# Dealing sums, weight products, LayerNorm and MLP steps out between tile products, and all of their transfers onto one queue in that order

## The chip, the cores and the metric

One core of a Trainium2 chip. The runs were made in batches, each on one chip with the kernel before beside it. The metric is the device time of one execution in microseconds, given as the median of the timed runs.

## The reference, cut to what matters

Two images of 256 channels, 128 x 128, float32. Three branches (dilations 1, 9, 12) each take offsets from a 3x3 convolution, sample the image bilinearly at 9 displaced taps, weight the samples per channel, sum, and apply LayerNorm and GELU. Their sum goes through a 1x1 convolution's addition, LayerNorm, a two-layer MLP and a second LayerNorm. A ternary 3x3 convolution follows.

```python
def _branch(x, w_off, w_def, lw, lb, pad, dil):
    off = _conv(x, w_off, pad, dil)
    y = _deform_dw(x, off, w_def, pad, dil)          # bilinear samples, 9 taps, summed
    return gelu(_ln2d(y, lw, lb))
x1 = _branch(x, off_w1, def_w1, bw1, bb1, 1, 1)
x2 = _branch(x, off_w2, def_w2, bw2, bb2, 9, 9)
x3 = _branch(x, off_w3, def_w3, bw3, bb3, 12, 12)
c = einsum('bchw,oc->bohw', x, conv_w) + conv_b
out = _ln2d(x1 + x2 + x3 + c, n1_w, n1_b)
h = gelu(out @ mlp_w1.T + mlp_b1) @ mlp_w2.T + mlp_b2
out = _ln2d(h + out, n2_w, n2_b)
# ... residual, group norm, ternary 3x3 convolution, residual
```

## The kernel before: the parts that matter

Sampling is a matrix product here: a tile of image rows (`xs`) times a matrix of interpolation weights (`A`). A is a product too: one factor is loaded by DMA straight into A, the other into `hy`, and VectorE (DVE) multiplies them in place. This is called a build below.

```python
def load_columns(u):                                 # A's first factor, 3 loads per unit
    for ky in taps(u):
        src, at, n = hat_rows(u, ky, TR, [[HY * 3 * W, TC], [0, TR]])
        pin(nc.scalar.dma_start(k["A"][u % 2][0:PT, AO + at : AO + at + n], src))

def build():                                         # A *= hy on DVE
    hy, u, at, n = hys.popleft()
    A = k["A"][u % 2][0:PT, AO + at : AO + at + n]
    pin(nc.vector.tensor_tensor(A, A, hy[0:PT, 0:n], ALU.mult))
    following = next(ahead, None)
    if following:
        load_rows(*following)                        # the next hy

def sample(u, c):                                    # unit u, channel half c
    # ...
    due = len(taps(u + 1)) if c == 0 and u + 1 < len(units) else 0
    last = c == KC - 1 and u + 2 < len(units)
    # ...
    ev = pool.tile([P, 9 * RI, NT * CI], F32, name="ev", tag="ev", bufs=2)
    for T in range(0, NT, 2):                        # 9 pairs of tiles
        if T // 2 % (NT // 2 // SLOTS + 1) == 0:     # at 3 places
            tail.advance()
        pm = psum.tile([P, 2, 256], F32, name="pm", tag="pm", bufs=4)
        # ... two products into pm on TensorE (PE), one copy pm -> ev on ScalarE (ACT)
    if last:
        load_columns(u + 2)
    sums = ev.rearrange("p (q i t) x -> p q i t x", q=3, t=3)
    for ky in kys:
        accumulate(u, c, sums, ky)                   # ring += w * ev on DVE, some 3 operations each
        for _ in range(due):
            build()                                  # unit u+1, after the first ky
        due = 0
```

A finished group of four rows goes through a chain of steps (transposes and statistics, normalising, transposing back, GELU, 1x1 convolution, MLP). Each chain is a generator; `yield n` asks to be continued at least n places later. `Tail.advance` is called at a place and runs one step of every chain that is due:

```python
def advance(self):
    self.now += 1
    # ... perhaps begin a waiting chain
    for item in list(self.running):
        if item[0] <= self.now and self.may(item):
            n = next(item[1], None)
            # ... remove the chain, or set item[0] = self.now + n
```

Three steps of a chain have a DVE operation that needs a result of PE or ACT from the same step:

```python
# normalised(): 4 transposes on PE, copied by ACT into T, then
nc.vector.bn_stats(st[:, j, :], Tv[:, j, :])
# finish(), first part: 1x1 convolution on PE into pc, then
nc.vector.scalar_tensor_tensor(S[:, m, :], pc, convb[:, m : m + 1], S[:, m, :], ALU.add, ALU.add)
# finish(), later: second MLP product on PE into h2, then
nc.vector.scalar_tensor_tensor(S[:, m, :], h2, b2[:, m : m + 1], S[:, m, :], ALU.add, ALU.add)
```

`pin` holds an instruction in program order on its engine; without it the scheduler may move it. Before, SyncE's transfers are not pinned.

## Time and profile before

| | before |
|---|---|
| time, median of 3 | 8016.15 us |
| sampling stage | 5779 us |
| PE busy in it, and idle | 5048, 731 us |
| DVE busy in it, and idle | 4536, 1243 us |
| PE waiting for ACT's copies | 565 us |
| DVE waiting for a finished sample | 862 us |

The stage rows come from the windows view, the waits from the groups by line; both are printed in the prediction. In the groups by line, the numbers after the bar are busy time and mean ns of one, then the idle time of the engine just before these instructions and what ended most of it.

```profile
L675 DVE TENSOR_TENSOR A<-A,hy 126x1152 f32<-126x1152 f32 (+2 forms) x752 | 970.9, 1342 | 37.9 <-DMA hy<-hats 20.8
```

The 752 builds cost DVE 971 us of work, and almost no waiting: their data is there when their turn comes.

### The profile page before, as it was taken

The numbers are of one execution on the slowest core, as the hardware profiler recorded it, in microseconds if no ns is written. First come the engines' busy times: TensorE is split into PE (matmuls) and PEld (weight loads), VectorE is DVE, ScalarE is ACT, GpSimd is POOL, SyncE is SP. The second block draws the span as 40 slices with busy tenths as digits, with TensorE's granted clock in tenths as the row PEclk, the third lists the DMA queues.
The fourth block names the chain that finished last, engine by engine and source line by source line (L and its number), as shares of the span: only waits on it lengthen the run. The fifth ranks groups of instructions, "written<-read, shape, count | busy, mean of one in ns | idle before, by whom it ended". The sixth has DMA issues, their size and how long they took to land. (4 is left out here: it accounts for less than half of the span.)

```text
span 7990.8 us, 100817 instructions
## 1 busy us (share of the span) xinstructions
PE 7025.9 (88%) x33648; PEld 5284.3 (66%) x33648; DVE 6010.1 (75%) x11183; ACT 4350.3 (54%) x8530; POOL 625.5 (8%) x1292
## 2 busy tenths in 40 slices
PE   5999878988888888888888898889888888699999
PEld 3555577777777777777677777777777776344444
DVE  7666578788778878877678778887787876577676
ACT  2344356666666666666656666666666666333232
POOL 0000000111111111111100111110111111000000
PEclk9999899999999999999999999999999999799999
DMA  8777677777677767766577767766776765222121
GB/s 299 208 194 192 172 245 242 220 233 230 222 219 220 234 213 227 229 213 204 181 230 239 226 220 230 234 220 217 226 226 213 233 213 160 75 81 73 69 79 49
DMA packets 833608, 1579.92 MB, mean 198 GB/s; under 512 B 96496, under 2 KB 492232, under 8 KB 828720
## 3 DMA queue, kind: packets, MB, share of 16 engines
q1 hardware_dynamic: 710384, 1106.97, 44.7%
q10 hardware_dynamic: 122688, 466.35, 18.5%
q8 instruction: 270, 4.42, 0.2%
q14 instruction: 266, 2.18, 0.1%
HBM read 1306.71 MB, written 266.36 MB: 197 GB/s over the span
## 5 line engine op out<-in xcount | busy, mean ns | idle before, releaser
L754 PE MATMUL pm<-A,xs 126*128 126x216 f32 (+2 forms) x17952 | 3570.0, 354 | 644.8 <-ACT ev L763 564.7
L754 PEld LDWEIGHTS pm<-A,xs 126*128 126x128 f32 x17952 | 3285.8, 199 | 922.2 <-ACT ev L763 688.3
L763 ACT COPY ev<-pm 128x432 f32<-128x432 f32 (+2 forms) x4752 | 2087.7, 492 | 1094.2 <-PE pm L754 709.1
L716 DVE SCALAR_TENSOR_TENSOR ring<-ev,defw,ring 128x384 f32<-128x384 f32 (+5 forms) x4376 | 2388.6, 568 | 130.6 <-ACT ev L763 28.5
L675 DVE TENSOR_TENSOR A<-A,hy 126x1152 f32<-126x1152 f32 (+2 forms) x752 | 970.9, 1342 | 37.9 <-DMA hy<-hats 20.8
L712 DVE TENSOR_SCALAR ring<-ev,defw 128x384 f32<-128x384 f32 (+2 forms) x568 | 305.8, 546 | 862.4 <-ACT ev L763 862.3
L480 ACT ACTIVATE T<-T,rs 128x256 f32<-128x256 f32 x1280 | 662.0, 599 | 6.8 <-POOL rs L476 6.8
L508 ACT ACTIVATE T<-zc,bb,bw 128x512 f32<-128x512 f32 x384 | 277.4, 774 | 621.4 <-DMA A<-hats 253.7
L1078 PE MATMUL pc<-cring,signs 128*128 128x512 bf16 x2304 | 520.9, 385 | 57.6 <-DVE signs L966 24.9
L1078 PE MATMUL pc<-cring,sums 128*128 128x512 bf16 x2304 | 510.3, 380 | 0.0
L473 POOL TENSOR_SCALAR rs<-mv 128x4 f32<-128x4 f32 x320 | 81.4, 254 | 5313.7 <-DVE mv L471 3889.3
L439 PE MATMUL hp<-T,w 128*128 128x512 f32 x1024 | 487.9, 600 | 9.1 <-ACT T L559 8.6
L469 DVE BATCH_NORM_STATS2 st<-T 128x6 f32<-128x256 f32 x1280 | 445.2, 411 | 59.1 <-ACT T L461 59.0
L203 PE MATMUL pz<-wz,xa 128*128 128x486 f32 x1024 | 459.1, 581 | 1.9 <-DVE zr L210 1.9
L439 PE MATMUL h<-hT,w 128*128 128x512 f32 x1024 | 460.0, 592 | 0.0
L1078 PEld LDWEIGHTS <-signs 128*128 128x128 bf16 x2304 | 227.1, 99 | 340.7 <-issue 44.4
L461 ACT COPY T<-tp 128x512 f32<-128x512 f32 x640 | 344.2, 597 | 196.8 <-PE tp L459 189.7
L1078 PEld LDWEIGHTS <-sums 128*128 128x128 bf16 x2304 | 225.4, 98 | 274.4
L492 PE MATMUL zc<-ident,T 128*128 128x128 f32 x2560 | 358.6, 287 | 29.9 <-ACT T L480 15.9
L492 PEld LDWEIGHTS zc<-ident,T 128*128 128x128 f32 x2560 | 319.1, 149 | 98.5 <-issue 39.6
L1062 ACT CAST cring<-D 128x2048 bf16<-128x2048 f32 x128 | 243.3, 1901 | 223.2 <-PE pc L1078 153.0
L572 ACT ACTIVATE hT<-hp,b 128x512 f32<-128x512 f32 x256 | 175.7, 687 | 339.2 <-PE hp L439 246.0
(119 smaller groups left out, 5722.7 us busy)
## 6 DMA issues: line engine op xcount, KB each, us to landing
A<-hats ACTq DMA_DIRECT2D x736, 567.0 KB
hy<-hats SPq DMA_DIRECT2D x736, 567.0 KB
xs<-table SPq DMA_DIRECT2D x1496, 126.0 KB
g12d<-T SPq DMA_DIRECT2D x128, 512.0 KB
other<-g12d SPq DMA_DIRECT2D x128, 512.0 KB
hats<-hb SPq DMA_DIRECT2D x192, 240.0 KB
hats<-hb SPq DMA_DIRECT2D x192, 192.0 KB
xl<-x1d SPq DMA_DIRECT2D x56, 640.0 KB
```

The lines of the kernel that those rows point to most:

```text
L203: nc.tensor.matmul(pz[:, 0:NZ], lhsT=xt[:, c, r, :], rhs=k["wz"][:, c, :], start=c == 0, stop=c == KC - 1,)
L439: nc.tensor.matmul(out, lhsT=w, rhs=v, start=i == 0, stop=i == n - 1)
L461: nc.scalar.copy(Tv[:, 2 * h : 2 * h + 2, :].rearrange("p j c -> p (j c)"), tp)
L469: pin(nc.vector.bn_stats(st[:, j, :], Tv[:, j, :]))
L480: nc.scalar.activation(Tv[:, j, :], Tv[:, j, :], AF.Identity, scale=rs[:, 0, j : j + 1], bias=rs[:, 1, j : j + 1],)
L492: nc.tensor.transpose(zc[:, j * P : (j + 1) * P], Tv[:, j, c * P : (c + 1) * P], ident)
L675: pin(nc.vector.tensor_tensor(A, A, hy[0:PT, 0:n], ALU.mult))
L712: pin(nc.vector.tensor_scalar(dst, src, w, None, ALU.mult))
L716: nc.vector.scalar_tensor_tensor(dst, src, w, dst, ALU.mult, ALU.add)
L754: nc.tensor.matmul(pm[:, j, 0:n], lhsT=xts[b, Rt][T + j][0:PT, c * P : (c + 1) * P], rhs=rhs, start=True, stop=True,)
L763: nc.scalar.copy(ev[:, q0 * 3 : q1 * 3, T * CI : (T + nt) * CI].rearrange("p m (t j) -> p t m j", j=CI), pm[:, 0:nt, 0:n].rearrange("p t ( ...
L1078: nc.tensor.matmul(pc[:, bank, :], lhsT=w[:, m * P : (m + 1) * P], rhs=xc[:, i, k, t * JC : (t + 1) * JC, kx : kx + W], start=j == 0, stop ...
```

## The change

The intent: PE, ACT and DVE should all have work between any two pairs of products, with no lump of sums and no several chain steps in one place. ACT should issue no transfers, so that its copies are never held. The core of the diff:

```diff
-NORMS = 3
+NORMS = 4
+XAHEAD = 4
-GAP = 2
-SLOTS = 3
+GAP = 4
         def advance(self):
-            for item in list(self.running):
+            for item in self.running:
                 if item[0] <= self.now and self.may(item):
                     ...
+                    return                          # one step of one chain
+        def load(self, tile, src):                  # every transfer of a chain
+            self.pin(nc.sync.dma_start(tile, src))
 ...  (load_columns)
-                pin(nc.scalar.dma_start(k["A"][u % 2][0:PT, AO + at : AO + at + n], src))
+                pin(nc.sync.dma_start(k["A"][u % 2][0:PT, AO + at : AO + at + n], src))
 ...  (load_rows)
-            nc.sync.dma_start(hy[0:PT, 0:n], src)
+            pin(nc.sync.dma_start(hy[0:PT, 0:n], src))
 ...  (sample, inside the loop over 9 pairs, after the products and the copy)
+                if following:                       # the next row tile's xs, pinned, one by one
+                    ...
+                            load_tile(*following, i + XAHEAD)
+                for _ in range(-(-len(pending) * 2 // (NT + 1 - T))):
+                    pending.popleft()()             # sums and builds of the sample before
+                tail.advance()                      # at all 9 places
 ...  (after the loop)
+            if kys:
+                pending.extend(sums(u, c, ev))
+            if c == KC - 1:
+                if u + 2 < len(units):
+                    load_columns(u + 2)
+                    pending.extend([build] * len(taps(u + 2)))
```

In the chains the waits grew (`yield 5` to `yield 8` before normalising, a new `yield 3` before the statistics, `yield 2` before both additions above, and others). A's load is issued at the end of a unit, and its build is dealt out within the very next sample, where before it came only after that sample, behind its first sums.

## The prediction

> **What bounds the kernel now.** I read the page's totals first, then the chain of waits, then the windows by stage.
>
> ```profile
> PE 7025.9 (88%) x33648; PEld 5284.3 (66%) x33648; DVE 6010.1 (75%) x11183; ACT 4350.3 (54%) x8530; POOL 625.5 (8%) x1292
> ...
> issue 7%; PE 6%; DVE 0%; DMA 0%; POOL 0%; POOLq 0%
> ```
>
> No engine is full, and the chain covers only the last stage (the 3x3 convolution). It says nothing of the stage that the change touches. Windows cut at the first and last tile product (953 and 6732 us) and at the last convolution's start do:
>
> ```profile
> core 0: us, PE busy (x) PEld busy (x) DVE busy (x) ACT busy (x) POOL busy (x), PEclk, DMA share, GB/s
> 0.00:953.00 953.00, 829.28 (x3400) 465.44 (x3400) 622.65 (x1345) 346.45 (x641) 3.42 (x9) 0.98 0.76 217
> 953.00:6732.00 5779.00, 5047.96 (x25159) 4291.42 (x25160) 4536.49 (x8706) 3591.71 (x7527) 589.85 (x1212) 0.95 0.71 222
> 6732.00:6904.00 172.00, 136.27 (x476) 73.27 (x474) 71.35 (x206) 95.68 (x171) 30.45 (x68) 0.88 0.25 80
> 6904.00:7991.00 1087.00, 1012.43 (x4616) 454.15 (x4616) 779.61 (x928) 316.46 (x192) 1.81 (x3) 0.96 0.20 71
> ```
>
> The second row is the sampling stage: 5779 us, 72% of the span. PE is idle for 5779 - 5048 = 731 us of it, DVE for 1243. The third row is the drain of the last chains. The stage has 2 images x 44 row tiles x 3 branches = 264 units of 2 samples (one per channel half), so 528 samples of 10.95 us. Each sample is 9 pairs of tile products, copied out by ACT, then summed by DVE.
>
> The groups by line and the waits say what PE and DVE wait for:
>
> ```profile
> L754 PE MATMUL pm<-A,xs 126*128 126x216 f32 (+2 forms) x17952 | 3570.0, 354 | 644.8 <-ACT ev L763 564.7
> L763 ACT COPY ev<-pm 128x432 f32<-128x432 f32 (+2 forms) x4752 | 2087.7, 492 | 1094.2 <-PE pm L754 709.1
> L716 DVE SCALAR_TENSOR_TENSOR ring<-ev,defw,ring 128x384 f32<-128x384 f32 (+5 forms) x4376 | 2388.6, 568 | 130.6 <-ACT ev L763 28.5
> L712 DVE TENSOR_SCALAR ring<-ev,defw 128x384 f32<-128x384 f32 (+2 forms) x568 | 305.8, 546 | 862.4 <-ACT ev L763 862.3
> L508 ACT ACTIVATE T<-zc,bb,bw 128x512 f32<-128x512 f32 x384 | 277.4, 774 | 621.4 <-DMA A<-hats 253.7
> ```
>
> PE waits for ACT to empty product banks (565 us), though ACT is busy only 62% of the stage. So ACT is late, not full. DVE waits for a finished sample before its first sum (862 us): it gets the sums in one lump. The timeline shows one such place:
>
> ```profile
> 3004.57 9.41 ACTq L663 DMA_DIRECT2D A<-hats  x3
> 3014.09 1.45 ACT L508 ACTIVATE T<-zc,bb,bw 128x512 f32<-128x512 f32 x2 [11.42 <-DMA A<-hats]
> 3015.99 8.72 PE L754 MATMUL pm<-A,xs 126*128 126x216 f32 x30 [8.42 <-ACT ev L763]
> ```
>
> ACT's own queue issues the A loads and is held for 9.4 us. ACT then copies nothing, PE fills its 4 banks and stands for 8.4 us. What follows is slow as well:
>
> ```profile
> 3003.90:3015.40 11.50, 3.67 (x23) 3.34 (x21) 8.77 (x19) 1.31 (x2) 2.02 (x4) 0.84 0.80 235
> 3016.00:3024.00 8.00, 8.00 (x28) 7.63 (x28) 1.05 (x4) 4.03 (x9) 0.00 (x0) 0.62 0.91 282
> ```
>
> In the eight microseconds after the gap PE is called busy throughout, but the granted clock is 0.62: 30 passes take 8.72 us (0.29 each). An undisturbed stretch at 3004.49 does 16 in 3.09 (0.19 each). A gap is paid twice.
>
> **What the Trainium skill says.** "TensorE: Matmul & The Clock Gate", section "Part 1: The HAM clock gate": an array idle for about 3.4 us falls to half clock and needs about as long again to get back. The trace agrees (0.62 after an 8.4 us gap). Same page, "Architectural detail": ACT and DVE are strict FIFOs. Hence one blocked entry in ACT's queue holds all copies, as the 11.42 us row shows. "DMA: Bandwidth & Descriptors", section "Issuing engines are not separate DMA queues": moving an issue to another engine saves sequencer time alone, not bandwidth. Here an A issue takes 0.79 us of ACT's queue, which the page does not count as busy. "Perfetto Trace Analysis", section "Optimization Strategy", recommends interleaving regimes with different limits. That is this change. The 40-slice row of DVE does not resolve the lumps, but in 5 us windows of this stage I find DVE over 95% busy in 56% of them, at a stage mean of 78%.
>
> **The change part by part.** No arithmetic is added. The built programs have the same number of products, transposes and DVE operations; only their order differs.
>
> 1. *A loads from ACT to SyncE.* 752 x 0.79 = 594 us of ACT's queue time go, with every hold like the one above. ACT's need falls from (3592 + 594)/5779 = 72% to 62%. SyncE gets 752 issues to its 752 hy (0.79), 1496 xs (0.79) and about 576 tail transfers (near 0.45): 3000 x 0.79 + 576 x 0.45 = 2630 us, half the stage. It has room, but is one ordered queue.
> 2. *Tail steps dealt singly.* Before, 3 places per sample each run one step of every chain that is due. In the program order 3988 of the 4752 places between product pairs held no chain work on PE, and some 260 held the work of two or more steps at once. Now there are 9 places per sample and one step in each: 1501 of 4752 have PE work, never two kinds. A group of 4 rows needs about 58 steps over three branches; 64 groups x 58 = 3712 steps in 4752 places (78%), so chains keep up and no burst is forced. The heaviest place has one hidden-layer product pair (4 passes x 0.43 = 1.7 us) and 0.75 us of tile products. ACT's heaviest is two normalisations (2 x 0.60) and a copy (0.52), within what four banks absorb (3 us of products).
> 3. *Sums dealt over the next sample.* Same 4944 operations of 0.55 to 0.57 us (2694 us) and 752 builds of A (1.34 us, 971 us). DVE's order now alternates sums with chain steps. The 862 us wait should fall to 100 to 250, and LayerNorm statistics no longer stand behind ten sums.
> 4. *NORMS 4, longer waits between steps, split h2.* Neutral in work.
>
> Sum. PE's need: 5048 us as recorded, of which the clock of 0.95 costs up to 5048 x 0.05 = 250. So its floor is near 4800 us (9.1 per sample), against DVE's 4536 (8.6), DMA's 0.71 x 5779 = 4100 (7.8) and ACT's 3592 (6.8). With four engines this close PE won't reach its floor. I take half of the clock loss back (130) and leave 370 of the 731 us idle: 5048 - 130 + 370 = 5288 us, 10.0 per sample. Total: 953 + 5288 + 172 + 1087 = 7500, plus the 25 us by which the timed runs exceed the profile's span (8016 against 7991): about 7525. I round to 7520, -6.2%.
>
> **The rivals.**
> - *DVE becomes the bound through late A loads.* A's three loads now go out at a unit's end and are built five to seven places into the next sample, 5 to 8 us later; before it was 10 us or more (issues around 3031, builds at 3042.8). Three loads of 567 KB at the queue's busy rate (466 MB in 18.5% of 7991 us, 315 GB/s) take 5.4 us after the issue, or 9 with company. DVE would stand 1 to 3 us per unit, 260 to 800 us over 264 units. DVE has 2 x 10.0 - 17.2 = 2.8 us spare per unit, so most is swallowed; if not, the stage ends at 5500 to 5600 us and the total near 7800. Against: A and hy waits of DVE are 38 us now.
> - *SyncE's ordered queue.* Every third unit it issues 17 xs (13.4 us) ahead of A, in samples of 10 us. Stores that wait for ACT or DVE stand in the same line. SyncE already waits 1774 us for builds and 1125 us for products. If this delays A or xs, PE waits for DMA instead of ACT: 7700 to 7900.
> - *Small waits remain and only places change.* PE's gaps of under 3 us add up to some 360 of 820 us by my reading of the timeline; if only the long ones go (460 us, drain included), the total is still near 7550 less the clock.
> - *Better than thought*: PE at 95% of its floor, 5050 us, total 7290.
>
> **Range and chances.** The middle two cases give 7500 to 7800, the best 7290; I say 7280 to 7760. Slower than 7856 (-2%) needs both rivals in full. Faster by over 2%: 0.92; within 2%: 0.06; slower: 0.02.
>
> **What would show it.** Right: the wait of ACT for A loads gone, PE's wait for ACT copies below 300 us, DVE's first-sum wait below 250, sampling stage near 5290 us with granted clock 0.97 or more, the other stages unchanged within 1%. Wrong: DVE waiting for A or hy by hundreds of us (first rival), PE waiting for xs (second), PE's wait for copies still above 500, or a drain well over 172 us because chains fell behind.

## The result, and the profile after

The kernel after is correct and took **8439.38 us** (median of 4, 8420.19 to 8455.38) against 8018.61 us for the kernel before (median of 4, 8011.98 to 8025.51). The ratio is 1.0524, 95% interval 1.0497 to 1.055: 5.2% slower, where 6.2% faster had been predicted.

The windows of the kernel after, cut at the same events, with the same columns as before:

```profile
0.00:959.00 959.00, 826.73 (x3400) 464.93 (x3400) 622.28 (x1345) 346.33 (x641) 3.43 (x9) 0.98 0.76 216
959.00:7139.00 6180.00, 5290.43 (x25166) 4323.65 (x25167) 4532.92 (x8709) 3649.76 (x7530) 770.12 (x1212) 0.93 0.67 207
7139.00:7331.00 192.00, 148.20 (x470) 77.40 (x469) 71.16 (x207) 95.57 (x168) 31.03 (x68) 0.81 0.24 76
7331.00:8419.00 1088.00, 1013.74 (x4614) 453.93 (x4614) 777.58 (x924) 316.52 (x192) 1.82 (x3) 0.96 0.19 71
```

The sampling stage grew by 401 us and the drain by 20; the other two stages moved by 6 and 1. DVE did the same work in the stage (4533 against 4536 us), so its idle time went from 1243 to 1647 us. PE's busy time rose by 242 us at a granted clock of 0.93 instead of 0.95: the same products, slower.

The groups by line of the kernel after:

```profile
L825 PE MATMUL pm<-A,xs 126*128 126x216 f32 (+2 forms) x17952 | 3774.0, 358 | 527.9 <-DMA xs<-table 256.2
L834 ACT COPY ev<-pm 128x432 f32<-128x432 f32 (+2 forms) x4752 | 2205.6, 484 | 1927.1 <-PE pm L825 1361.4
L723 DVE TENSOR_TENSOR A<-A,hy 126x1152 f32<-126x1152 f32 (+2 forms) x752 | 989.7, 1342 | 841.2 <-DMA A<-hats 707.7
L770 DVE TENSOR_SCALAR ring<-ev,defw 128x384 f32<-128x384 f32 (+2 forms) x568 | 307.4, 548 | 378.6 <-ACT ev L834 377.7
```

PE's largest wait is now for its image tiles (256 us, 20 before), not for ACT's copies. DVE's first-sum wait fell from 862 to 379 us as the change intended. But the builds, which waited 38 us, now wait 841 us, 708 of them for A's load. What DVE saved in one place it lost in another, and more.

One such place in the timeline, SyncE's queue first. The columns are start, duration, engine and line, the operation, and how many in a row:

```profile
2341.94 5.06 SPq L685 DMA_DIRECT2D xs<-table  x6
...
2348.56 9.63 SPq L685 DMA_DIRECT2D xs<-table  x11
...
2358.86 3.46 SPq L711 DMA_DIRECT2D A<-hats  x3
...
2363.00 0.88 SPq L447 DMA_DIRECT2D xn<-in_x  x1
```

DVE at that time (in brackets: idle before, and what ended it):

```profile
2349.47 4.78 DVE L777 SCALAR_TENSOR_TENSOR ring<-ev,defw,ring 128x357 f32<-128x357 f32 x8
2365.81 1.36 DVE L723 TENSOR_TENSOR A<-A,hy 126x1152 f32<-126x1152 f32 x1 [11.55 <-DMA A<-hats]
2368.37 1.36 DVE L723 TENSOR_TENSOR A<-A,hy 126x1152 f32<-126x1152 f32 x1 [1.20 <-DMA A<-hats]
```

ACT (the last copy of the sample that ran meanwhile, and the scaling of xn) and PE, a little later:

```profile
2361.05 0.34 ACT L834 COPY ev<-pm 128x216 f32<-128x216 f32 x1 [0.46 <-PE pm L825]
...
2374.43 0.81 ACT L568 ACTIVATE xn<-xn,shift,gn_rstd 128x512 f32<-128x512 f32 x1 [10.67 <-DMA xn<-in_x]
...
2375.30 2.93 PE L453 MATMUL pc<-xn,convw 128*128 128x512 f32 x3 [9.46 <-ACT xn L568]
```

Seventeen xs issues go out first. A's three follow at 2358.86, and the first of them is built at 2365.81, 7 us later. DVE's queue stands 11.55 us at that build. The sums behind it were ready when the sample's last copy ended, at 2361.39, and could not pass; for the first 7 us of the stand they were not ready either. PE stands 9.46 us soon after, but not for DVE: it waits for xn, whose load SyncE issued at 2363.00, behind the xs and A.

Not every unit has such a place. Only at every third unit, where the row tile changes, do the 17 xs stand ahead of A. I matched each of the 752 builds in the trace with its A issue: in these 88 units DVE stands 758 of the 841 us (8.6 us a unit), in all the others together 84 us (0.5 us a unit).

### The profile page after: what moved, and what is told of

It reads as the page before. It is cut to its first block, busy times and chain, and to the rows that moved or that the text cites. A ratio compares the mean times of both kernels' runs of the same rounds, so it can differ in the third digit from the quotient of the medians.

```text
span 8418.4 us, 100644 instructions
## 1 busy us (share of the span) xinstructions
PE 7279.1 (86%) x33648; PEld 5319.9 (63%) x33648; DVE 6003.9 (71%) x11183; ACT 4408.2 (52%) x8530; POOL 806.4 (10%) x1292
## 5 line engine op out<-in xcount | busy, mean ns | idle before, releaser
L825 PE MATMUL pm<-A,xs 126*128 126x216 f32 (+2 forms) x17952 | 3774.0, 358 | 527.9 <-DMA xs<-table 256.2
L834 ACT COPY ev<-pm 128x432 f32<-128x432 f32 (+2 forms) x4752 | 2205.6, 484 | 1927.1 <-PE pm L825 1361.4
L502 ACT ACTIVATE T<-T,rs 128x256 f32<-128x256 f32 x1280 | 700.3, 600 | 142.5 <-POOL rs L496 134.8
L493 POOL TENSOR_SCALAR rs<-mv 128x4 f32<-128x4 f32 x320 | 161.6, 505 | 5557.8 <-DVE mv L491 3998.1
L517 PE MATMUL zc<-ident,T 128*128 128x128 f32 x2560 | 468.0, 306 | 194.6 <-ACT T L502 188.3
L453 PE MATMUL hp<-T,w 128*128 128x512 f32 x1024 | 512.1, 622 | 44.5 <-ACT T L597 42.1
L453 PE MATMUL h<-hT,w 128*128 128x512 f32 x1024 | 479.4, 592 | 0.0
L479 ACT COPY T<-tp 128x512 f32<-128x512 f32 x640 | 376.8, 593 | 103.2 <-PE tp L477 100.0
L495 POOL TENSOR_TENSOR rs<-rs,mhalf 128x4 f32<-128x4 f32 x320 | 377.4, 1179 | 0.0
L453 PE MATMUL pc<-xn,convw 128*128 128x512 f32 x512 | 271.7, 654 | 100.0 <-ACT xn L568 100.0
```

The costliest lines, as they stand in the source:

```text
L453: nc.tensor.matmul(out, lhsT=w, rhs=v, start=start and i == 0, stop=stop and i == n - 1)
L479: nc.scalar.copy(Tv[:, 2 * h : 2 * h + 2, :].rearrange("p j c -> p (j c)"), tp)
L495: nc.gpsimd.tensor_tensor(rs[:, 0, :], rs[:, 0, :], mhalf[:, 0:NB4], ALU.pow)
L502: nc.scalar.activation(Tv[:, j, :], Tv[:, j, :], AF.Identity, scale=rs[:, 0, j : j + 1], bias=rs[:, 1, j : j + 1],)
L517: nc.tensor.transpose(zc[:, j * P : (j + 1) * P], Tv[:, j, c * P : (c + 1) * P], ident)
L825: nc.tensor.matmul(pm[:, j, 0:n], lhsT=xts[b, Rt][T + j][0:PT, c * P : (c + 1) * P], rhs=rhs, start=True, stop=True,)
```

## The experiments

Sixteen more kernels were run, each beside the kernel before on the same chip in the same rounds; the medians of the kernel before lay between 8009 and 8026 us throughout, so a difference of up to some 20 us between two batches says nothing. Intervals are given where the text leans on them. Results are correct except for one kernel.

| run | what it is | us | ratio (95%) |
|---|---|---|---|
| after | the whole change | 8439 | 1.0524 (1.0497 to 1.055) |
| e1_A_on_ACT | after, A loads back on ACT | 8374 | 1.043 (1.041 to 1.0451) |
| e2_build_later | after, builds a sample later | 8119 | 1.013 (1.0105 to 1.0154) |
| e3_A_aside | after, builds do not use the load (wrong result) | 8075 | 1.0063 |
| e4_before_A_on_SP | before, only A loads on SyncE | 7793 | 0.9712 (0.9696 to 0.9728) |
| e5_sums_lump | after, sums and builds in a lump as before | 8611 | 1.0755 |
| e6_old_tail | e2, chains as before | 8064 | 1.0063 |
| e7_free_SP | e2, hy and chain transfers not pinned | 8009 | 1.0001 (0.9969 to 1.0034) |
| e8_longer_waits | e2, longer waits inside chains | 8115 | 1.0122 |
| e9_sums_early | e7, sums done in the first four places | 8123 | 1.0141 |
| e10_e4_sums_dealt | e4, sums and builds dealt out | 8004 | 0.9994 (0.9977 to 1.0011) |
| e11_e4_single_steps | e4, single chain steps at 9 places | 8472 | 1.0576 |
| e12_e4_xn_later | e4, one chain wait longer by 2 | 7676 | 0.9586 (0.957 to 0.9602) |
| e13_e10_h2_later | e10, second addition a place later | 8008 | 0.9988 |
| e14_e7_DVE_later | e7, three DVE steps 3 places later | 7885 | 0.9846 (0.982 to 0.9872) |
| e16_e12_h2_later | e12, second addition a place later | 7708 | 0.9634 |
| e17_e13_all_later | e10, three DVE steps a place later | 7815 | 0.9758 (0.9728 to 0.9788) |

### First question: the builds, or the queue?

The first theory was that DVE's wait for A (841 us) lengthens the stage: DVE stands, so sums, `ev` buffers, copies and products come late. The rivals: SyncE's ordered queue delays everything on it, or chain steps come too soon after their producers. The first four kernels were to tell these apart.

**A loads back on ACT.**

```diff
-                pin(nc.sync.dma_start(k["A"][u % 2][0:PT, AO + at : AO + at + n], src))
+                pin(nc.scalar.dma_start(k["A"][u % 2][0:PT, AO + at : AO + at + n], src))
```

> The changed kernel with one part undone: the A loads are issued by ACT again, at the same place of the order. Theory 1 (the A loads land too late for their builds; DVE stood 841 us for them, and that is what made the sampling stage 401 us longer): the loads no longer stand behind 17 xs issues and the hy issues that wait for builds, so DVE's wait at the builds falls below 500 us, against new holds of ACT's queue; 8000 to 8250 us. Theory 2 (the single steps stand too close after what they need, so that PE waits in its own order for ACT and DVE, and its clock falls; DVE's wait is slack): within 1% of 8439. Theory 3 (the one ordered queue of SyncE as such delays everything on it, xs too): near 8000, with PE's wait for xs down from 256 us to under 60.

It took 8374 us, only 65 less than after. Its waits:

```profile
DVE A L723 <- DMA A<-hats: 377.8, 242, 8.1
...
ACT ev L834 <- DMA A<-hats: 300.1, 43, 13.4
```

(Total us, times, longest.) The loads go out earlier and DVE waits 330 us less for them, but ACT is held again for 300. One stand was exchanged for the other. By its own forecasts the run speaks for theory 2 (within 1% of 8439), which the next run contradicts; alone it does not decide.

**Builds one sample later.** The load stays where it is; its build moves to nearly where it was in the kernel before (three sums earlier).

```diff
+            if c == 0 and 0 < u < len(units) - 1:
+                pending.extend([build] * len(taps(u + 1)))
             if kys:
                 pending.extend(sums(u, c, ev))
             if c == KC - 1:
                 if u + 2 < len(units):
                     load_columns(u + 2)
-                    pending.extend([build] * len(taps(u + 2)))
```

> The changed kernel with the three builds of a unit moved one sample later (from the places 5 to 7 after the A loads are issued to the first places of the next sample, some 10 us after the issue); the loads stay on SyncE. Theory 1: DVE's wait at the builds falls from 841 us to under 200 and the time to 7650 to 8000. Theory 2: the wait falls but the time stays within 1.5% of 8439, as the idle time moves to other waits. Theory 3: PE's wait for xs stays near 256 us, time 8200 to 8400.

8119 us: 320 less than after, from the place of the builds alone. PE's wait for xs fell from 256 to 180 us as well. But DVE still waits 430 us for A, the kernel is still slower than before, and none of the three forecasts was met. Of the 485 us that DVE stands at builds here for any cause, 406 are again in the units with xs ahead of A.

**A's load taken out of the build.** The load goes to scratch memory in DRAM, and the build multiplies hy by itself. The result is wrong (relative error 0.615); the number of builds and loads is unchanged.

```diff
+                if u > 1:
+                    gone = k["gone"][u % 2][ky + 1]
+                    pin(nc.sync.dma_start(gone[0:PT, 0:n], src))
+                    continue
 ...
-            pin(nc.vector.tensor_tensor(A, A, hy[0:PT, 0:n], ALU.mult))
+            other = A if u < 2 else hy[0:PT, 0:n]
+            pin(nc.vector.tensor_tensor(A, other, hy[0:PT, 0:n], ALU.mult))
```

> Wrong results on purpose. The A loads keep their size, source, queue and place but land in DRAM scratch, so that no build waits for them; the build multiplies the hy tile by itself. Theory 1: DVE's wait at the builds below 100 us, time 7500 to 7900, the gain that the prediction had counted on. Theory 2: time stays at 8250 or more without the wait. Theory 3: between, 8000 to 8250, with PE waiting for xs by 200 us or more.

8075 us. From the groups by line (without the two builds that still use the load):

```profile
L728 DVE TENSOR_TENSOR A<-hy 126x1152 f32<-126x1152 f32 (+1 forms) x750 | 969.1, 1339 | 0.0
...
L775 DVE TENSOR_SCALAR ring<-ev,defw 128x384 f32<-128x384 f32 (+2 forms) x568 | 308.2, 550 | 733.2 <-ACT ev L839 732.2
```

With the wait gone altogether the change gets 364 us back, hardly more than by moving the builds, and is still 0.6% slower than before. So the builds are the largest single loss, yet not all that is wrong: of the gain that was the reason for the change, nothing is to be seen. DVE now waits 732 us for `ev`, 378 in after: its idle time in the stage fell by 328 us only (1647 to 1319), though some 820 us of stand at builds are gone. So more than half of that stand was time in which DVE would have stood elsewhere. The forecast that was met is theory 3's (8000 to 8250, PE's wait for xs over 200; it is 280). (Writing to DRAM instead of on-chip memory may have an effect of its own. Nor does SyncE have to wait any more until PE has released A: 859 us in after, at L711, none here. The run does not separate these.)

So it is both: the build set close behind the load (e2), and the xs ahead of A that make the load late. The second is read from the trace; e1, which takes A out of that queue, cuts the wait by 330 us, but no run keeps A on SyncE and issues it ahead of the xs.

**Only the A loads, in the kernel before.** One word:

```diff
-                pin(nc.scalar.dma_start(k["A"][u % 2][0:PT, AO + at : AO + at + n], src))
+                pin(nc.sync.dma_start(k["A"][u % 2][0:PT, AO + at : AO + at + n], src))
```

> The kernel before with one part of the change alone: its A loads are issued by SyncE instead of ACT. If the holds of ACT's queue cost what the prediction said, and SyncE has room: ACT's 254 us wait for A loads goes and the time falls to 7750 to 7950. Theory 3: SyncE's queue holds the A loads behind others, builds wait by over 200 us, time 8000 to 8200. Theories 1 and 2 say nothing against the first, since builds there come 13 us after the issue.

7793 us, 2.9% faster than before. Its sampling stage, by windows:

```profile
963.00:6553.00 5590.00, 4973.82 (x25160) 4235.78 (x25160) 4539.24 (x8705) 3640.74 (x7528) 598.30 (x1212) 0.95 0.75 229
```

PE's wait for ACT's copies fell from 565 to 295 us, and ACT's wait for A loads is gone. This one word is the part of the change that pays, and everything else in the change then costs 646 us (8439 - 7793).

### Second question: which of the other parts costs the rest?

**Sums in a lump again**, with builds after the first three sums, as before; single chain steps and SyncE's order stay.

```diff
-            if kys:
-                pending.extend(sums(u, c, ev))
+            steps = list(sums(u, c, ev)) if kys else []
+            if c == 0 and 0 < u < len(units) - 1:
+                steps[3:3] = [build] * len(taps(u + 1))
+            for step in steps:
+                step()
```

> The changed kernel with the dealing of the sums undone: all sums of a sample stand in DVE's order right after the sample, with the next unit's builds after the first three of them, as in the kernel before; the single chain steps and all loads on SyncE in the program's order stay. If the dealing of sums is what costs against the kernel before with its A loads on SyncE (7793 us): 7750 to 7900. If the single chain steps cost it: 8050 or more, as for the changed kernel with later builds (8119). If both share it: between.

8611 us, the slowest of all. The lump is not to be had back by itself. DVE's longest wait is for the finished sample again:

```profile
DVE ring L770 <- ACT ev L834: 1059.6, 281, 14.5
```

**The chains of before** in the kernel with later builds: three places, every due step, transfers of the chains not pinned, old waits.

```diff
-NORMS = 4
+NORMS = 3
-GAP = 4
+GAP = 2
-            for item in self.running:
+            for item in list(self.running):
 ...
-                    return
 ...  (normalised, branch and finish as in the kernel before)
```

> The changed kernel with later builds, and the dealing of chain steps undone: three places a sample, every chain that is due steps there, with the old waits; the chains' own loads and stores are free in SyncE's order again as before. Sums stay dealt over the next sample. If single chain steps cost: 7750 to 7900. If the dealing of sums costs: 8050 or more.

8064 us, 55 less than e2. Single steps are then not what holds this kernel; and since chain transfers were freed as well, the 55 us may belong to these (the next kernel, which frees them and keeps single steps, is faster still).

**SyncE's order given up** for hy loads and chain transfers (xs and A stay in order):

```diff
         def load(self, tile, src):
-            self.pin(nc.sync.dma_start(tile, src))
+            nc.sync.dma_start(tile, src)
 ...
-            pin(nc.sync.dma_start(hy[0:PT, 0:n], src))
+            nc.sync.dma_start(hy[0:PT, 0:n], src)
```

> The changed kernel with later builds, but the hy loads and the chains' transfers are no longer held to the program's order on SyncE (xs and A loads still are). If the ordered queue is what makes xs and A late (PE's wait for xs 180 us, DVE's for A 430 us): both fall by half and the time to 7800 to 7950. If it isn't: within 1% of 8119.

8009 us, 110 less than e2, so the ordered queue does cost something. DVE's wait for A stayed at 409 us (430 in e2), so those remaining waits are not what the 110 us were. PE's wait for xs fell from 180 to 138 us.

**Longer waits inside the chains.** PE waits 157 us for transposing back (zc) and 118 us for the 1x1 convolution's input in e2; three waits were made longer.

```diff
-            yield 2, None, KC
+            yield 5, None, KC
-            yield 10
+            yield 16
-            yield 2, None, 1
+            yield 5, None, 1
```

> The changed kernel with later builds, and three of the waits between chain steps longer: 2 to 5 places from the normalisation to the transposes back, 2 to 5 from the scaled input to the 1x1 convolution, 10 to 16 from its load to its use. If PE stands because the steps follow too close on what ACT and the loads give them: PE's waits for the normalised tile (157 us) and for xn (118 us) fall to under 60 together and the time to 7850 to 8000. If these waits only stand where PE would wait anyhow: within 1% of 8119.

8115 us, no gain (e2: 8119). The waits themselves nearly vanished. Two of PE's waits (total us, times, longest):

```profile
PE pm L825 <- ACT ev L834: 291.2, 232, 5.7
...
PE zc L517 <- ACT T L502: 25.4, 13, 4.6
```

PE's wait for zc went from 157 to 25 us, but its wait for copies went from 154 to 291 and ACT's wait for `ev` buffers (that is, for DVE) from 568 to 692. PE was not what set the pace, so its idle time only moved. That points at DVE.

**Sums finished earlier.** Perhaps DVE releases `ev` too late because the sums are spread over the whole next sample; here three go in each place, so that they end in the first four.

```diff
-                for _ in range(-(-len(pending) * 2 // (NT + 1 - T))):
+                for _ in range(min(3, len(pending))):
```

> The changed kernel with later builds and free hy and chain transfers (8009 us), with the sums and builds dealt three to a place, so that a sample's sums end in the first four of the next sample's nine places instead of the last. Slack theory (dealt to the last place, the sums free the ev buffer only when ACT already needs it, so every stand of DVE passes to ACT and PE): ACT's wait for the ring sums falls from 560 us to under 300 and the time to 7800 to 7950. If slack in ev doesn't matter: within 1% of 8009, the waits only change names.

8123 us, 1.4% slower than e7, which neither forecast has. ACT's wait for sums fell only from 560 to 476 us, not below 300: the edit hardly gave the slack, so the theory of too little slack in `ev` is weakened, not settled.

### Third question: what does dealing out cost DVE?

Two kernels add one part each to e4, the fast base.

**Sums and builds dealt out over the next sample**, chains and SyncE as in e4:

```diff
+                for _ in range(-(-len(pending) * 2 // (NT + 1 - T))):
+                    pending.popleft()()
 ...
-            for ky in kys:
-                accumulate(u, c, sums, ky)
-                for _ in range(due):
-                    build()
-                due = 0
+            for j, ky in enumerate(kys):
+                pending.extend(sums(u, c, ev, ky))
+                if j == 0:
+                    pending.extend([build] * due)
```

> The kernel before with its A loads on SyncE (7793 us) and one more part alone: sums and builds dealt over the next sample's nine places; chain steps in three places, SyncE's order free, as before. Slack theory: ACT's wait for ring sums rises from 376 us to over 600 and the time to 7950 to 8100. If dealing is harmless by itself and only the ordered loads and single steps cost: 7700 to 7850.

8004 us: dealing out the sums alone gives back 211 us of e4's 225. DVE's waits in e4, then in e10 (total us, times, longest):

```profile
DVE ring L712 <- ACT ev L763: 438.0, 198, 8.0
...
DVE T L587 <- PE h L439: 201.2, 69, 11.7
DVE st L469 <- ACT T L461: 166.1, 69, 9.1
...
DVE T L549 <- PE pc L439: 37.3, 9, 16.6
```

```profile
DVE T L587 <- PE h L439: 489.1, 126, 11.1
DVE st L469 <- ACT T L461: 276.3, 131, 13.6
...
DVE ring L722 <- ACT ev L795: 169.8, 89, 8.0
DVE T L549 <- PE pc L439: 130.1, 86, 16.4
```

The wait for the sample did fall, 438 to 170. But the waits at three chain steps (MLP addition, statistics, convolution's addition) rose from 201 + 166 + 37 = 404 to 489 + 276 + 130 = 895. The four together rose by 223 us, close to the 211 in the time. In a lump the sums are a cushion: while DVE works them off, PE and ACT finish the chain step, and DVE comes to its part late. Dealt out, DVE is soon at the chain step, finds it unfinished, and the ready sums stand behind it. At this point that is argued: the forecast of the slack theory (7950 to 8100) came true as well, with ACT's wait for sums up from 376 to 582 us. The fourth question tests it.

**Single chain steps at nine places** on e4, sums in a lump:

```diff
+            for item in self.running:
 ...
+                    return
 ...  (normalised, branch and finish as in the kernel after, transfers not pinned)
+            tail.advance()                          # at all 9 places
```

> The kernel before with its A loads on SyncE and the other part alone: one chain step at each of nine places with the new waits; sums in a lump, SyncE's order free. If single steps need dealt sums (a step's DVE work now stands behind up to ten sums while PE's next step is two places off): 8200 or more, near the 8611 of the changed kernel with its sums in a lump. If that 8611 came from the ordered loads: 7750 to 7900.

8472 us, 679 more than e4, with DVE's wait for the sample at 870 us and a stage clock of 0.92. Single steps without dealt sums are the worst combination, as e5 had shown from the other side. Why it is so bad was read in the waits only, not taken apart.

**One chain wait longer on e4.** A look at whether the base can do better: the image tile `xn` used six places after its load, not four.

```diff
-            yield 4
+            yield 6
```

> The kernel before with its A loads on SyncE and the wait between the xn load and its use raised from 4 to 6 places. PE stood 149 us for xn in the kernel with A on SyncE alone. If that wait is on the path that sets the end: 7640 to 7740. If it only moves to another: within 1% of 7793.

7676 us, 4.1% faster than before, correct, and the fastest kernel. PE's wait for the convolution's input fell from 149 to 41 us, and DVE's wait for the sample from 438 to 195. The first alone does not cover the stage's 139 us (5590 to 5451).

### Fourth question: is it the chain steps on DVE?

If DVE's stands at chain steps are the cause, setting those steps later must recover the loss.

**One of three later, on e10** (the MLP addition, one of the three places in a sample):

```diff
+                yield 1
                 pin(
                     nc.vector.scalar_tensor_tensor(
                         S[:, m, :], h2, b2[:, m : m + 1], S[:, m, :], ALU.add, ALU.add
```

> The kernel before with A on SyncE and sums dealt (8004 us), with one place more between the second MLP product and DVE's addition of it. If DVE's stands at chain steps (with ready sums behind them in its order) are what dealing costs: DVE's wait for that product falls from 489 us to under 200 and the time by 100 to 250 us, to 7750 to 7900. If they are only where DVE would stand anyhow: the wait falls and the time stays within 1% of 8004.

8008 us, unchanged. DVE's waits of this run:

```profile
DVE st L469 <- ACT T L461: 488.5, 172, 11.7
DVE T L549 <- PE pc L439: 338.1, 106, 14.4
...
DVE T L588 <- PE h L439: 126.1, 68, 11.5
```

The chosen wait fell from 489 to 126 us, and the other two rose from 406 to 827. By its forecast the run speaks for a DVE that would stand anyhow; the other reading, that the stand moved to the next step that was too close, needs the last run below.

**Three DVE steps later on e7**: statistics 3 to 6 places, both additions 2 to 5.

```diff
-            yield 3                # ahead of the statistics
+            yield 6
-                yield 2
+                yield 5
-                yield 2
+                yield 5
```

> The changed kernel with later builds and free hy and chain transfers (8009 us), with the three waits ahead of DVE's chain steps longer (second MLP product and 1x1 convolution 2 to 5 places, statistics 3 to 6). If the stands cost: DVE's wait for the product falls from 438 us to under 200 and the time to 7750 to 7900. If not: within 1% of 8009.

7885 us, 124 less than e7. The wait for the MLP addition fell from 438 to 204. DVE's wait for A stayed at 411, and yet the time fell: a wait total by itself does not say what it costs.

**The MLP addition later on e12**, the same `yield 1`:

```diff
+                yield 1
                 pin(
                     nc.vector.scalar_tensor_tensor(
                         S[:, m, :], h2, b2[:, m : m + 1], S[:, m, :], ALU.add, ALU.add
```

> The fastest kernel so far (before, A on SyncE, xn 6 places ahead: 7676 us), with one place more between the second MLP product and its addition. DVE stood 252 us for that product there. If such a stand is on the path also with sums in a lump: 7500 to 7620. If DVE has slack there: within 1% of 7676.

7708 us, no gain over 7676. Here too the stand moved on: DVE's wait at the convolution's addition rose from 169 to 285 us.

**All three later on e10**: e13 with the same `yield 1` ahead of the statistics and of the convolution's addition.

```diff
             self.read.add(what)
+            yield 1                                 # ahead of the statistics
 ...
+                yield 1                             # ahead of the convolution's addition
                 pin(
                     nc.vector.scalar_tensor_tensor(
                         S[:, m, :], pc, convb[:, m : m + 1], S[:, m, :], ALU.add, ALU.add
```

> As e13 (the kernel before with A on SyncE, sums dealt, the second MLP product's addition one place later), with DVE's statistics and the addition of the 1x1 convolution one place later too. If DVE's stands at chain steps are what the dealing costs: the three waits (126, 488 and 338 us in e13) fall to under 400 together and the time by over 100 us, to 7700 to 7900. If standing DVE isn't the cause: the waits fall and the time stays within 1% of 8008.

7815 us: 189 of e10's 211 us are back (8004 - 7815). Its DVE waits and its stage:

```profile
DVE T L590 <- PE h L439: 83.6, 38, 17.3
DVE st L470 <- ACT T L461: 75.0, 49, 6.1
...
DVE T L551 <- PE pc L439: 20.8, 20, 2.4
```

```profile
955.00:6526.00 5571.00, 4946.06 (x25142) 4173.62 (x25143) 4529.98 (x8701) 3581.36 (x7517) 770.30 (x1212) 0.96 0.75 230
```

The three waits total 179 us (953 in e13), and the stage is as short as e4's. ACT still waits 532 us for sums (582 in e10), so slack in `ev` is not what made the difference. The cost of dealing out the sums was these stands; one of three was not enough (e13), all three together were. Dealing out brings no gain over e4 even then. Not tried: the three later steps on e4 itself, with sums in a lump. If they help there too, part of the 189 us is not owed to the dealing; e16, one later step on a lump, gained nothing.

## Why the prediction was wrong

The runs make a path from before to after, each step a difference of medians, with up to some 20 us of uncertainty where the two runs are of different batches:

| step | us | shown by |
|---|---|---|
| A loads from ACT to SyncE | -225 | e4 against before |
| sums and builds dealt over the next sample | +211 | e10 against e4 |
| single chain steps, xs one by one and in order, builds three sums earlier | +5 | e7 against e10 |
| hy and chain transfers held in order on SyncE | +110 | e2 against e7 |
| builds in the sample right after the load's issue | +320 | after against e2 |
| sum | +421 | 8439 - 8018 |

The +5 is within that uncertainty, and it is the sum of several edits that may cancel. The parts interact (single steps cost 679 on a lump of sums, 5 here), so another path would share them out otherwise.

**What held.** Step 1: the hold of ACT by its own A issues was real, and its removal worth 225 us. No arithmetic was added; the first and last stages are the same within 1%; chains kept up (the drain grew from 172 to 192 us). PE's wait for copies fell to 131 us, below the forecast 300.

**The step that failed: the first rival was spread over all units and set aside.** The prediction worked out that DVE would stand "1 to 3 us per unit, 260 to 800 us over 264 units" at builds, then wrote "DVE has 2 x 10.0 - 17.2 = 2.8 us spare per unit, so most is swallowed", and its sum has no term for it. The stand was 841 us, but not of that form: 758 us of it in the 88 units with 17 xs ahead of A, 8.6 us each, three times the spare time; 0.5 us each in the others. So the short way from load to build made little stand by itself. It met the queue of the second rival in the same units, and the prediction had kept the two apart. What it cost is 320 us by moving the builds (e2) and 364 us without the wait (e3): so a little more than half of the stand was swallowed, and the rest, over 300 us, is what the sum left out. That ready sums stand behind a build is seen in the place shown; that `ev`, ACT's copies and PE's products follow from there is argued. The remark "A and hy waits of DVE are 38 us now" was no evidence against it: that figure belonged to the old place of the builds and to A's old queue.

**The arithmetic of that rival was wrong too.** Of the case that it is not swallowed it says "the stage ends at 5500 to 5600 us": 5288 plus 260 to 800 is 5548 to 6088, a total of 7785 to 8325 us. The whole of this rival lay outside the stated range, which ends at 7760. In the terms of the prediction's sum for the stage, 5048 - 130 + 370: PE's busy time rose by 242 us where it should have fallen by 130, and PE's idle time is 890 us, not 370.

**The landing estimate was sound, the issue was not.** The prediction took 5.4 to 9 us from issue to landing; the place shown had 7 us. A unit's end was not the time of issue, though, where xs went first.

**The second rival was true as well.** It made A late, as above, and xs too: PE's wait for xs rose from 20 to 256 us. Holding hy and chain transfers in order costs 110 us of the time (e2 against e7); it explains only 42 us of the wait for xs (180 in e2, 138 in e7).

**A cost was missed.** "The 862 us wait should fall to 100 to 250": it fell to 379 us, and the time did not follow, because DVE then stands at chain steps whose PE or ACT part is not done. The third rival, that small waits remain and "only places change", comes nearest, but costs it at 30 us (7550 against 7520). It is worth +211 us (e10), and e17 shows its cause. The sum of the prediction counted the first-sum wait as a gain and gave nothing against it.

**The clock** was forecast at 0.97 or more in the stage and was 0.93. Adding up (1 - clock) x PE busy over 5 us windows of the stage, I get 340 us lost against 231 before. PE's gaps of 3 us and more in the stage total 453 us after and 398 before, the shorter ones 436 and 333 (the prediction had read some 360 of 820). How much of the loss is owed to which stays open. At the gap that the prediction shows, the clock record has half clock from 4.3 us into the gap to 6.1 us after the products resume, so getting back took longer there than the 3.4 us that it quotes.

Open too: why single steps on a lump of sums cost 679 us; what the lateness of xs costs by itself; and what is gained by issuing A ahead of the xs, which no run tries. The 410 to 430 us that e2, e7 and e14 still wait for A are no riddle: of what DVE stands at their builds, 406 of 485, 391 of 461 and 440 of 479 us lie in the units with xs ahead.

## What to carry to other kernels

Move a blocked DMA issue off an engine that also does the work in between: that one word was worth 2.9%, and the tested kernel that adds only a longer chain wait (e12) beats both versions here by 4% and 9%. Don't count an engine's idle share as room for a new wait when its queue is in order and others depend on what stands behind; compare the new distance from issue to use with the measured landing time first, count what stands ahead of the issue in its queue, and do it for each kind of unit, not for the mean. When work is dealt out finely, place every step that needs another engine's result far enough behind that result, move all such steps together, and try each part of the change alone before all of them at once.

## What the Trainium skill lacked or had wrong

- "DMA: Bandwidth & Descriptors", section "Issuing engines are not separate DMA queues", says that issuing from another engine only saves the sequencer's time, "usually small relative to the DMA itself". Here moving 752 issues from ACT to SyncE, and nothing else, saved 225 us of 8018 (e4). What went is the 0.79 us of each issue and also ACT's copies standing behind an issue that waits (9.41 us for three in the prediction's timeline, where three free ones take 2.4); the run does not separate the two. The page lacks the second.
- "Perfetto Trace Analysis", section "Optimization Strategy", recommends interleaving regimes. It lacks the condition: interleaved sums took away a cushion, and steps too close behind their producers then stopped ready work, +211 us (e10). One later step changed nothing (e13), all three together gave 189 us back (e17).
- No page that I read says what holding transfers of different kinds in program order on one engine's queue can cost: +110 us here for hy and chain transfers (e2 against e7), and 758 of DVE's 841 us at builds in the units where 17 small loads were issued ahead of A.
